# Edge step 1 of a graph network in four stages instead of three, with more buffers for the streams of step 0

## The chip, the cores and the metric

The kernel runs on one core of a Trainium2 chip. The metric is the device time in microseconds (us) of one execution. A core has five engines with their own instruction queues: TensorE (PE in the profile, and PEld for its weight loads), VectorE (DVE), ScalarE (ACT), GpSimd (POOL) and SyncE (SP). They run side by side and wait for each other through semaphores. In this kernel SP starts the plain transfers, and POOL starts the gathers, which fetch rows of a table by index.

## The reference

The network has 12,500 nodes and 412,500 edges, sorted by destination. Two graph convolutions come first; this change doesn't touch them. Then a mesh network runs: nodes and edges are encoded to 64 features, and two edge steps, each followed by a node step, update them. Cut to what matters here:

```python
e = _ln(_mlp(edge_feat, edge_enc_w0, ...))                 # edge encoder
for s in range(2):
    ce = concat([e, n[senders], n[receivers]])
    e = e + _ln(_mlp(ce, edge_blk_w0[s], edge_blk_b0[s], edge_blk_w1[s], edge_blk_b1[s]))
    agg = segment_sum(e, receivers)
    n = n + _ln(_mlp(concat([n, agg]), node_blk_w0[s], ...))
# _mlp(x) = silu(x @ w0 + b0) @ w1 + b1;  _ln is a layer norm over 64 features
```

## The kernel before

The edges are padded to 405 groups of 1,024 (8 tiles of 128). An edge step is a loop of three iterations on the device, and each iteration has 135 groups unrolled in it. `edge_step(s)` writes out, by hand, the order of the instructions on PE, DVE and ACT (`manual_schedule` names these three). SP's order is left to a planner; POOL issues the gathers in the order of the program.

For one group c the work has these stages.

- **Loads.** `send` brings the encoder's input `at` (step 0, L894) or the stored edge features `e` (step 1, L950). `send_window` brings, in four transfers of SP, the receivers' table rows `qd` (L958) and the relative destinations `rb` (L959). `ahead` has POOL issue eight gathers of 128 rows of the senders' table (L348) into the ring buffer `pg`. The ring has five buffers (R = 5), and the gathers run three groups ahead (LA = 3), so in step g POOL writes the buffer that the hidden layer of group g-2 read.
- **Hidden layer.** `hidden_blk` multiplies `e` and the receivers' part (L908) and adds the gathered rows (L910) in one PSUM bank; ACT applies Silu and writes `h` (L913). In step 0 `hidden_enc` does the same for the encoder (L899, L901).
- **Output layer.** `second` adds the bias (L918) and multiplies `h` by the second weights (L920). `normalised` squares on ACT (`sq`, L419), sums on DVE (`var`, L421), takes a reciprocal root in eleven small DVE operations (L422, L403 to L408) and scales into `y` (L427).
- **Window sum.** `window_sum` multiplies `y` by a one-hot matrix `oh` (L318) on PE (L330). DVE adds the 64-node window to the accumulator in the next step (L338).

The constants `ENC, ENC2, TURN, BLK, BLK2, SUM` say how many steps after a group's first step each stage is issued. Step 0 also encodes, so it has six stages, and in it the outputs of the encoder and of the block go through one `normalised` call with two parts (tile `sq16`). In step 1, `BLK, BLK2, SUM` are 0, 1, 2. In step g, PE therefore gets, in this order: the output layer of group g-1, the window sum of group g-2, the hidden layer of group g. ACT gets `sq` of group g-1 and then `h` of group g. DVE gets the pending window addition, the one-hot matrices `oh` and `ot` (L965), and the normalisation of group g-1.

Of the kernel before, what the change touches and what calls it, by code (L numbers as in the profile page):

```python
# [9 lines left out]
F32 = mybir.dt.float32  # L10
# [8 lines left out]
P = 128  # L19
K = 8  # L20
W = 64
D = 64
# [13 lines left out]
def gcn_then_mesh_gnn_kernel(ctx: ExitStack, tc: tile.TileContext, a: dict, out: bass.AP):  # L36
# [28 lines left out]
    KP = K // 2  # L65
# [24 lines left out]
    def bank(name):  # L90
        return psum.tile([128, 512], F32, name=f"ps_{name}")
# [23 lines left out]
    with tc.tile_pool(name="prep", bufs=2) as prep:  # L115
        ldst = prep.tile([P, NT], I32, name="ldst", bufs=1)
        nc.sync.dma_start(ldst, a["dstT"])
        for g0 in range(0, NG, P):
            n = min(P, NG - g0)
# [46 lines left out]
    with tc.tile_pool(name="sort", bufs=1) as sp, \  # L166
# [116 lines left out]
        for t, to in ((free, slot_t), (k, drel_t), (vals[turn], ew_t)):  # L283
            for j0 in range(0, NS, 4):
                n = min(4, NS - j0)
# [113 lines left out]
    def rsqrt(pool, v, shape, name):  # L399

        y = pool.tile(shape, F32, name=f"{name}_y")
        t = pool.tile(shape, F32, name=f"{name}_t")
        nc.vector.tensor_single_scalar(t.bitcast(I32), v.bitcast(I32), 1, op=OP.arith_shift_right)  # L403
        nc.vector.tensor_scalar(y.bitcast(I32), t.bitcast(I32), -1.0, MAGIC, op0=OP.mult, op1=OP.add)
        for _ in range(3):
            nc.vector.tensor_mul(t, y, y)  # L406
            nc.vector.scalar_tensor_tensor(t, t, -0.5, v, op0=OP.mult, op1=OP.mult)  # L407
            nc.vector.scalar_tensor_tensor(y, t, 1.5, y, op0=OP.add, op1=OP.mult)  # L408
        return y

    def normalised(pool, n, *parts):


        k = parts[0][0].shape[1] // D
        m = len(parts) * k
        sq = pool.tile([n, m, D], F32, name=f"sq{m}")
        v = pool.tile([n, m], F32, name=f"var{m}")
        for i, (o, _) in enumerate(parts):
            nc.scalar.activation(sq[:, i * k:(i + 1) * k, :], o.rearrange("p (k f) -> p k f", f=D),  # L419
                                 AF.Square, scale=D ** -0.5)  # L420
            nc.vector.tensor_reduce(v[:, i * k:(i + 1) * k], sq[:, i * k:(i + 1) * k, :], axis=AX.X, op=OP.add)  # L421
        nc.vector.tensor_scalar_add(v, v, EPS)  # L422
        r = rsqrt(pool, v, [n, m], f"rs{m}")
        for i, (o, y) in enumerate(parts):
            s = r[:, i * k:(i + 1) * k, None]
            o = o.rearrange("p (k f) -> p k f", f=D)
            nc.vector.tensor_tensor(y, o, s.to_broadcast(list(y.shape)), op=OP.mult)  # L427
# [25 lines left out]
    with tc.tile_pool(name="gcn", bufs=1) as gp, tc.tile_pool(name="gcnw", bufs=2) as gw:  # L453
# [209 lines left out]
        for c in range(NCH):  # L663
# [6 lines left out]
            h = gw.tile([32, CN], F32, name="h")  # L670
# [31 lines left out]
    work = first.enter_context(tc.tile_pool(name="first", bufs=2))  # L702
# [114 lines left out]
    def node_mlp(products, b0, w1, b1, update):  # L817

        ph = bank("h")
        for i, (w, v) in enumerate(products):  # L820
            nc.tensor.matmul(ph[:D, :CN], w, v, start=(i == 0), stop=(i == len(products) - 1))  # L821
        h = work.tile([D, CN], F32, name="nh")
        nc.scalar.activation(h, ph[:D, :CN], AF.Silu, bias=b0)  # L823
        po = bank("o")
        nc.tensor.matmul(po[:NP, :CB * D], ones[:, :NP], b1, start=True, stop=False)
        for b in range(CB):
            nc.tensor.matmul(po[:NP, b * D:(b + 1) * D], h[:, b * NP:(b + 1) * NP], w1[:D, :D],  # L827
                             start=False, stop=(b == CB - 1))
        y = work.tile([NP, CB, D], F32, name="ny")
        normalised(work, NP, (po[:NP, :CB * D], y))  # L830
        pt = bank("t")
        for b in range(CB):
            nc.tensor.transpose(pt[:D, b * NP:(b + 1) * NP], y[:, b, :], ident[:NP, :NP])  # L833
        update(pt[:D, :CN])
# [55 lines left out]


    def edge_inputs(col):
        at = work.tile([16, KP * P], F32, name="at")
        nc.sync.dma_start(at, a["attrT"][:, ds(col, KP * P)])  # L894
        return at

    def hidden_enc(at):
        ph = bank("h")
        nc.tensor.matmul(ph, ee_w0, at, start=True, stop=True)  # L899
        h = work.tile([128, KP * P], F32, name="h")  # L900
        nc.scalar.activation(h, ph, AF.Silu, bias=ee_b0)  # L901
        return h

    def hidden_blk(s, e, pg, more=()):

        ph = bank("h")
        for i, (w, v) in enumerate([(eb_w0[s], e), *more]):
            nc.tensor.matmul(ph, w, v, start=(i == 0), stop=False)  # L908
        for j in range(KP):
            nc.tensor.matmul(ph[:, j * P:(j + 1) * P], pg[:, 2 * j:2 * j + 2, :].rearrange("p k f -> p (k f)"),  # L910
                             ident, start=False, stop=(j == KP - 1))
        h = work.tile([128, KP * P], F32, name="h")
        nc.scalar.activation(h, ph, AF.Silu, bias=eb_b0[s])  # L913
        return h

# [15 lines left out]
    def edge_step(s):  # L931
# [2 lines left out]
        ring = [work.tile([P, K, D], F32, name=f"pg{i}", bufs=1) for i in range(R)]  # L934
        acc = (s01, 0, 128) if s == 0 else (ns2, D, D)

        ENC, ENC2, TURN, BLK, BLK2, SUM = (0, 1, 2, 3, 4, 5) if s == 0 else (None, None, None, 0, 1, 2)

        def body(it, drl, offs, ahead):
            feats, hids, hidb, y0, y1, es, windows, hots, ohs = ({} for _ in range(9))  # L940
# [3 lines left out]
            def send(g):  # L944

                if s == 0:
                    feats[g] = edge_inputs(col(g))
                else:
                    es[g] = work.tile([128, KP * P], F32, name="e", bufs=6)
                    nc.sync.dma_start(es[g], e1_d[:, ds(col(g), KP * P)])  # L950
# [22 lines left out]
            for g in range(GB + SUM + 1):  # L973
# [24 lines left out]
                if parts:  # L998
                    normalised(work, P, *parts)
# [13 lines left out]
                if s == 0 and real(g):  # L1013
                    hids[g] = hidden_enc(feats.pop(g))
                if real(g - BLK):
                    c = g - BLK
                    hidb[c] = hidden_blk(s, es[c], ring[c % R], hots.pop(c))
# [7 lines left out]
    def spread_edge_step(s):  # L1025
        def body(it, group):
# [10 lines left out]
            for g in range(GI):  # L1037
                gs = slice(g * K, (g + 1) * K)
                col = (it * GI + g) * (KP * P)
                pg = work.tile([P, K, D], F32, name="pg")  # L1040
                qg = work.tile([P, K, D], F32, name="qg")
                gather(tabs_p[s], si[:, gs], pg)
                gather(tabs_q[s], di[:, gs], qg)
                nc.vector.tensor_add(pg, pg, qg)
                e = work.tile([128, KP * P], F32, name="e")
                if s == 0:
                    y0 = ys[:, 0, gs, :]
                    normalised(work, P, (second(hidden_enc(edge_inputs(col)), *ee1), y0))
                    nc.scalar.activation(e, turned(y0), AF.Identity, scale=e_g[0])
                    y = ys[:, 1, gs, :]  # L1050
                else:
                    nc.sync.dma_start(e, e1_d[:, ds(col, KP * P)])
                    y = ys[:, gs, :]
                normalised(work, P, (second(hidden_blk(s, e, pg), *eb1[s]), y))
                if s == 0:
                    nc.vector.scalar_tensor_tensor(e, turned(y), e_g[1], e, op0=OP.mult, op1=OP.add)
                    nc.sync.dma_start(e1_d[:, ds(col, KP * P)], e)
                group(g, val)
# [8 lines left out]
    for s in range(2):  # L1067
        with tc.tile_pool(name=f"edges{s}", bufs=2) as work:
            edge_step(s)
        with tc.tile_pool(name=f"spread{s}", bufs=2) as work:  # L1070
            spread_edge_step(s)
        with tc.tile_pool(name=f"nodes{s}", bufs=2) as work:
            for c in range(NCH):
                node_step(s, c)
                if s == 0:
                    send_tables(1, c)
                else:
                    decode(c)
# [45 lines left out]
```

## Time and profile before

| what | value |
|---|---|
| three runs, median | 18249.7 us (18242.7 to 18254.52) |
| profiled execution: its own time, its span | 18269.4 us, 18267.6 us |
| mean granted TensorE clock | 0.804 |
| edge step 0 with its loads | about 6020 to 12420 us |
| edge step 1 with its loads | about 12750 to 17780 us |
| share of the span: PE, PEld, DVE, POOL, ACT | 70%, 53%, 50%, 34%, 13% |

The profile describes one execution. A row of its costliest groups gives the line, the engine, the operation, what it writes and reads, how often it ran, its busy time and mean duration, and then the idle time of that engine just before it with what ended most of that idle time. "remote" as what ended a wait means that a semaphore moved, but that no instruction or transfer in the profile ended near that moment; on one core it is not another core. "issue" means that the profile shows no wait at all. The ends of matmuls are modelled, not observed.

### The profile page before, as it was taken

To read this page: it belongs to the slowest core of one execution; us is meant where nothing else is said; L and a number is where in the kernel's file an instruction comes from. 1 tells how busy PE (TensorE), PEld (TensorE's weight loads), DVE (VectorE), ACT (ScalarE), POOL (GpSimd) and SP (SyncE) were. 2 spreads that over 40 slices of the span, in tenths; PEclk is the share of its full clock that TensorE was granted. 3 is DMA by queue.
4 is the path that set the end of the run, shared out by engine and by line. 5 is a ranking of instruction groups with operands and counts; after the bars stand their busy time and mean duration, and the time that the engine had idled before them with its cause. 6 is when DMAs were issued, how large, how long until landed. Compare 5 with 4: busy or idle time off the path is not lost. (4 is left out here: it accounts for less than half of the span.)

```text
span 18267.6 us, 286566 instructions
## 1 busy us (share of the span) xinstructions
PE 12803.6 (70%) x107075; PEld 9720.4 (53%) x107682; DVE 9165.7 (50%) x23663; ACT 2363.3 (13%) x3705; POOL 6263.8 (34%) x6572
## 2 busy tenths in 40 slices
PE   0179999899995677777777777777555555555556
PEld 0169999699994444454444444443434343433432
DVE  9967777577775344444444444443333333333332
ACT  3300000000001112222222122221111111111110
POOL 0000000000000444454444444441666666666650
PEclk9989999899995777777777777775777777777775
DMA  0011111111111112221212222222222222222230
GB/s 25 7 13 61 58 56 56 42 56 57 53 62 27 46 46 48 47 52 47 46 46 47 49 48 48 48 48 45 61 58 58 59 58 58 58 58 58 58 51 2
DMA packets 1008981, 877.55 MB, mean 48 GB/s; under 512 B 650695, under 2 KB 755755, under 8 KB 1006879
## 3 DMA queue, kind: packets, MB, share of 16 engines
q1 hardware_dynamic: 798640, 644.15, 12.1%
q0 software_dynamic: 208896, 214.33, 7.4%
q8 instruction: 884, 14.48, 0.3%
q14 instruction: 561, 4.59, 0.1%
HBM read 723.20 MB, written 134.51 MB: 47 GB/s over the span
## 5 line engine op out<-in xcount | busy, mean ns | idle before, releaser
L348 POOL DMA_INDIRECT pg<-tab_p,si_cur x6480 | 6209.5, 958 | 5153.3 <-PE ps_h L910 2936.8
L920 PE MATMUL ps_o<-eb_w,h 128*128 128x128 f32 x6480 | 1193.0, 340 | 2167.0 <-ACT h L913 1639.6
L552 PE MATMUL ps_h<-t,roh 128*128 128x128 bf16 x39936 | 2541.4, 220 | 234.4 <-DVE roh L531 234.4
L552 PEld LDWEIGHTS <-roh 128*128 128x128 bf16 x39936 | 2395.3, 99 | 284.1 <-DVE roh L531 238.3
L421 DVE TENSOR_REDUCE var<-sq 128x8 f32<-128x512 f32 (+1 forms) x1290 | 857.5, 668 | 2943.5 <-ACT sq L419 2118.8
L920 PEld LDWEIGHTS ps_o<-eb_w,h 128*128 128x128 f32 x6480 | 1008.1, 237 | 2384.6 <-ACT h L913 1748.7
L330 PE MATMUL ps_seg<-oh,y 128*64 128x64 f32 x19440 | 1482.8, 250 | 1017.3 <-issue 993.4
L348 POOL DMA_INDIRECT pg<-tab_p,si_fst x48 | 45.5, 947 | 5452.9 <-DVE offs L368 5438.9
L568 PE MATMUL ps_seg<-ohd,msg 128*128 128x112 f32 x13312 | 1850.4, 280 | 0.0
L330 PEld LDWEIGHTS ps_seg<-oh,y 128*64 128x64 f32 x19440 | 1199.8, 160 | 1155.2 <-issue 1113.2
L965 DVE TENSOR_SCALAR ot<-rb,iop 128x512 bf16<-128x512 bf16 x810 | 303.4, 375 | 2657.0 <-DMA rb<-relg_d 2224.2
L568 PEld LDWEIGHTS ps_seg<-ohd,msg 128*128 128x128 f32 x13312 | 1628.2, 192 | 0.0
L559 DVE TENSOR_TENSOR msg<-ps_h,wm 128x512 f32<-128x512 f32 (+1 forms) x1792 | 1166.2, 651 | 722.8 <-PE ps_h L552 711.8
L908 PE MATMUL ps_h<-e,eb_w 128*128 128x512 f32 x1620 | 1401.1, 954 | 147.7 <-issue 82.1
L910 PEld LDWEIGHTS ps_h<-ident,pg 128*128 128x128 f32 x6480 | 1108.7, 241 | 252.9 <-issue 162.3
L556 DVE TENSOR_TENSOR ohd<-ior,rdrel 128x448 f32<-128x448 f32 (+1 forms) x1792 | 1056.3, 590 | 276.0 <-PE ps_seg L568 249.0
L913 ACT ACTIVATE h<-ps_h,eb_b 128x512 f32<-128x512 f32 x810 | 556.4, 687 | 4865.1 <-remote 2996.3
L910 PE MATMUL ps_h<-ident,pg 128*128 128x128 f32 x6480 | 1086.8, 322 | 39.2 <-issue 35.6
L419 ACT ACTIVATE sq<-ps_o 128x512 f32<-128x512 f32 (+1 forms) x1290 | 754.2, 585 | 2148.4 <-issue 680.3
L899 PE MATMUL ps_h<-at,ee_w 16*128 16x512 f32 x810 | 703.4, 928 | 426.4 <-issue 351.8
L908 PEld LDWEIGHTS <-qd 128*128 128x128 bf16 x2430 | 306.7, 127 | 1022.8 <-issue 973.5
L427 DVE TENSOR_TENSOR y<-ps_o,rs_y 128x512 f32<-128x512 f32 x1215 | 802.3, 687 | 89.9 <-issue 4.1
(247 smaller groups left out, 12454.2 us busy)
## 6 DMA issues: line engine op xcount, KB each, us to landing
mod<-mod_d SPq DMA_DIRECT2D x256, 832.0 KB
pg<-tab_p,si_cur POOLq DMA_INDIRECT x6480
rb<-relg_d SPq DMA_DIRECT2D x1620, 64.0 KB
e_d<-e SPq DMA_DIRECT2D x405, 256.0 KB
e<-e_d SPq DMA_DIRECT2D x405, 256.0 KB
qd<-tab_q SPq DMA_DIRECT2D x1620, 24.0 KB
at<-in_attrT SPq DMA_DIRECT2D x405, 32.0 KB
tab_q<-tabs SPq DMA_DIRECT2D x50, 187.5 KB
```

What stands on the lines that cost most here:

```text
L330: nc.tensor.matmul(ps[r:r + n, :W], v, oh[:, k, :], start=(k == 0), stop=(k == K - 1))
L348: nc.gpsimd.indirect_dma_start(out=to[:, k, :], out_offset=None, in_=table, in_offset=bass.IndirectOffsetOnAxis(ap=idx[:, k:k + 1], axis=0))
L419: nc.scalar.activation(sq[:, i * k:(i + 1) * k, :], o.rearrange("p (k f) -> p k f", f=D), AF.Square, scale=D ** -0.5)
L421: nc.vector.tensor_reduce(v[:, i * k:(i + 1) * k], sq[:, i * k:(i + 1) * k, :], axis=AX.X, op=OP.add)
L427: nc.vector.tensor_tensor(y, o, s.to_broadcast(list(y.shape)), op=OP.mult)
L552: nc.tensor.matmul(pg[:, (j - j0) * SB * F:(j - j0 + 1) * SB * F], ohs[h][:, u, at * P:(at + 1) * P], t3[:, i, u, b:b + SB * F], start=(i ...
L556: nc.vector.tensor_tensor(ohd[:, :n, :], ior[:, None, :].to_broadcast([P, n, LR]), drel[:, j0:j0 + n, r:r + 1].to_broadcast([P, n, LR]), o ...
L559: nc.vector.tensor_tensor(msg[:, :n * SB, :], pg[:, :n * SB * F].rearrange("p (s f) -> p s f", f=F), wm[:, j0:j0 + n, :].rearrange("p j s ...
L568: nc.tensor.matmul(acc[:SB * F, :LR], msg[:, j * SB:(j + 1) * SB, :].rearrange("p s f -> p (s f)"), ohd[:, j, :], start=(j0 + j == 0), sto ...
L908: nc.tensor.matmul(ph, w, v, start=(i == 0), stop=False)
L910: nc.tensor.matmul(ph[:, j * P:(j + 1) * P], pg[:, 2 * j:2 * j + 2, :].rearrange("p k f -> p (k f)"), ident, start=False, stop=(j == KP - 1))
L920: nc.tensor.matmul(po[:, j * 128:(j + 1) * 128], h[:, j * P:(j + 1) * P], w1, start=False, stop=(j == KP - 1))
```

## The change

The changed kernel does three things.

- In edge step 1 the stages become `BLK, BLK2, SUM = 0, 2, 3`. In step g, PE gets the output layer of group g-2, the window sum of group g-3 and the hidden layer of group g. The loop over steps is one longer in each of the three iterations.
- The tile `h` gets three buffers instead of two, in both functions that allocate it, since two hidden layers now wait while a third is written.
- The encoder's input `at` (used in step 0 alone) gets four buffers instead of two, and the squares of a two-part call (`sq16`, step 0 alone) get one instead of two. The squares of a one-part call keep two.

```diff
-        sq = pool.tile([n, m, D], F32, name=f"sq{m}")
+        sq = pool.tile([n, m, D], F32, name=f"sq{m}", bufs=1 if m > K else 2)
...
-        at = work.tile([16, KP * P], F32, name="at")
+        at = work.tile([16, KP * P], F32, name="at", bufs=4)
...
     def hidden_enc(at):
...
-        h = work.tile([128, KP * P], F32, name="h")
+        h = work.tile([128, KP * P], F32, name="h", bufs=3)
...
     def hidden_blk(s, e, pg, more=()):
...
-        h = work.tile([128, KP * P], F32, name="h")
+        h = work.tile([128, KP * P], F32, name="h", bufs=3)
...
-        ENC, ENC2, TURN, BLK, BLK2, SUM = (0, 1, 2, 3, 4, 5) if s == 0 else (None, None, None, 0, 1, 2)
+        ENC, ENC2, TURN, BLK, BLK2, SUM = (0, 1, 2, 3, 4, 5) if s == 0 else (None, None, None, 0, 2, 3)
```

## The prediction

> **What bounds the kernel now.** I read the slices of the page first: edge step 0 fills about 6020 to 12420 us of the span and edge step 1 about 12750 to 17780 us. The stages change only in step 1, so I asked for the busy times in three stretches inside its iterations. The columns are PE, PEld, DVE, ACT and POOL, each with its count, then clock, DMA share and GB/s:
>
> ```profile
> 13000.00:14400.00 1400.00, 765.61 (x4275) 561.62 (x4331) 528.22 (x1935) 145.46 (x227) 881.73 (x909) 0.75 0.26 58
> 14500.00:16000.00 1500.00, 827.04 (x4569) 604.23 (x4631) 563.69 (x2066) 156.37 (x244) 945.39 (x975) 0.75 0.26 58
> 16200.00:17700.00 1500.00, 806.21 (x4542) 594.40 (x4602) 562.58 (x2057) 155.88 (x243) 942.91 (x970) 0.76 0.27 58
> ```
>
> The reader is to see the pace. 909 + 975 + 970 = 2854 gathers in 4400 us are 356.75 groups of eight, so a group takes **12.33 us**, 405 of them 4994 us. No engine is full: POOL is busiest, at 63%.
>
> Then the groups of instructions between 13000 and 17700 us (379 groups of edges):
>
> ```profile
> L348 POOL DMA_INDIRECT pg<-tab_p,si_cur x3032 | 2943.6, 971 | 1719.5 <-issue 800.2 <-PE ps_h L910 462.6 <-remote 446.7
> L920 PE MATMUL ps_o<-eb_w,h 128*128 128x128 f32 x3036 | 657.3, 384 | 2037.3 <-ACT h L913 1547.5 <-issue 469.6 <-ACT sq L419 20.1
> L913 ACT ACTIVATE h<-ps_h,eb_b 128x512 f32<-128x512 f32 x379 | 260.3, 687 | 3213.4 <-remote 2746.2 <-PE ps_h L910 256.0 <-issue 190.0
> ```
>
> PE stands idle 2037.3 / 379 = **5.38 us** per group ahead of the output layer, waiting for `h`; its other work takes 12.33 - 5.38 = 6.95 us. POOL stands idle 1719.5 us ahead of gathers. The ordinary gap between two gathers is 0.30 us (the timeline below), 910 us over 3032, so 810 us or **2.14 us** per group are real pauses. POOL's own pace without them is 12.33 - 2.14 = 10.2 us.
>
> Why `h` is late is in the timeline:
>
> ```profile
> 15513.61 1.40 POOL L348 DMA_INDIRECT pg<-tab_p,si_cur  x1 [2.25 <-remote]
> 15514.30 2.08 PE L920 MATMUL ps_o<-eb_w,h 128*128 128x128 f32 x8 [5.66 <-ACT h L913]
> 15516.30 1.97 PE L330 MATMUL ps_seg<-oh,y 128*64 128x64 f32 x16
> 15520.86 1.05 PE L910 MATMUL ps_h<-ident,pg 128*128 128x128 f32 x8
> ...
> 15531.53 0.69 ACT L913 ACTIVATE h<-ps_h,eb_b 128x512 f32<-128x512 f32 x1 [14.52 <-remote]
> ...
> 15532.27 2.07 PE L920 MATMUL ps_o<-eb_w,h 128*128 128x128 f32 x8 [10.04 <-ACT h L913]
> ...
> 15538.38 1.05 PE L910 MATMUL ps_h<-ident,pg 128*128 128x128 f32 x8
> 15539.04 0.94 POOL L348 DMA_INDIRECT pg<-tab_p,si_cur  x1 [5.08 <-PE ps_h L910]
> ```
>
> The hidden layer's matmuls are over at 15521.9, but ACT may start only at 15531.53: 9.6 us later, with nothing else in its way. Over the trace these late releases come only when POOL has issued gathers for some 6 us without a pause; the lag averages 4.9 us a group in step 1 and 0.1 us in step 0, where POOL rests 6 us a group. So a pause of POOL lets PE's releases through, and PE's release lets POOL go on. At 15531.5 the chain `h`, output, sum, hidden layer (7.5 us) runs before POOL's next release at 15539.04: that is the 5.08 us pause.
>
> **What the Trainium skill says.** "Perfetto Trace Analysis", section "Tensor Engine Instruction (MATMUL, LD_WEIGHTS)": the end of a matmul is an estimate, and the semaphore is sent only after PSUM has acknowledged the write. The trace agrees that a modelled end is no release, but at 15539.53 ACT starts 0.10 us after the last L910 (15538.38 + 1.05), so the 9.6 us are no acknowledgement. The same page, "DMA Instruction — SWDGE (GPSIMD)": a gather's interval ends with its descriptors, not with the data. So POOL's 0.94 us is issuing time; in this stretch the data is not late (waits for `pg` sum to under 4 us). "TensorE: Matmul & The Clock Gate", "What's actually happening": after an idle window of about 3.4 us the array runs at half clock. The trace agrees: the eight matmuls of L920 take 2.08 us after a 5.66 us wait, but 1.16 us at 15540.27 after a 0.52 us wait.
>
> **The change part by part.**
>
> *Output layer one step later.* PE still issues the same instructions per group. The wait of 5.38 us ahead of L920 loses its cause: `h` of group g-2 was started a whole step earlier. Of the 5.38 us ACT itself takes 0.7; the rest is late release. If nothing took its place, PE would need 6.95 us a group, and POOL would bound. What the program can gain is therefore POOL's pauses at most: 2.14 x 405 = 867 us.
>
> Which pauses go? I counted POOL's runs between pauses over 0.8 us, from 12800 to 17700 us: 195 runs of eight gathers followed by a pause of 2.29 us on average (12.1 us a group); 51 runs of sixteen followed by 4.48 us; and 39 runs of fourteen and two, with pauses of 1.22 and 4.84 us. These hold 3000 of some 3130 gathers. The long pauses are the chain above, 7.5 us after a late release. With the change the next hidden layer doesn't wait for `h`, and so has mostly been done by the time the release comes; I shorten these to the 2.29 us of the short ones: 51 x (4.48 - 2.29) + 39 x (1.22 + 4.84 - 2.29) = 112 + 147 = **259 us**. The 2.29 us pauses I leave, since they are what lets a release through, not PE's work. Bounds: no gain (0), and all pauses gone (867).
>
> *Window sum one step later.* It stays one step behind the output layer. It needs `y`, so ACT `sq` 0.60, `var` 0.69, eleven small operations at 0.20, `y` 0.69: 4.2 us, and 1.26 us of L338, L318 and L965, which DVE does first: 5.5 us. Between the two PE now has a sum, a hidden layer and an output layer, about 6.9 us. It fits by 1.4 us; a release of L920 that is late by 4.9 us would make PE wait 3.5 us there. That keeps PE at 10.5 us a group, near POOL's 10.2, so I charge nothing, and hold the rest in the rivals.
>
> *One step more at the end of each iteration*: three times at most PE's 6.95 us, **+21 us**. Its loads and gathers are not more.
>
> *`h` with three buffers* follows the later reader; no instruction changes. Cost 0.
>
> *`at` with four buffers (step 0).* SP waits there for L899, 3045 us (and 871 "remote") in the queue's own waits, and `qd`, `rb` stand behind it; DVE waits 2119.6 us for `rb` ahead of L965. These waits go. In the order built from the changed kernel the store of `e` comes ahead of the last `rb` load of a window, two steps ahead of its use. But PE is what orders step 0: its whole wait for DVE's `y` is under 30 us there, and DVE's next work, `var`, waits for PE's outputs anyway (`ot` at 9509.81, `sq` on ACT at 9510.60, `var` at 9511.23). Value 0; if that cover fails, 0.15 us a group either way, ±60 us.
>
> *`sq16` with one buffer (step 0).* The next square comes some 14 us after the last reduction of the old one (9512.86 and 9527.84). Cost 0, and up to 405 x 0.1 = 40 us if ACT were made to wait.
>
> *Sum*: -259 + 21 = **-238 us**. Against the profiled execution's 18269.4 us this gives 18031; it stands 20 us above the median, so against the median 18249.7 - 238 = **18012 us**.
>
> **The rivals.**
>
> *A. Pauses go more widely.* PE gets a group or more ahead, releases are always there in time, and half or all of the 2.29 us pauses vanish as well: another 195 x 2.29 / 2 = 223 us and more, so 17400 to 17790. For it: PE's 6.95 us against 10.2. Against it: without pauses no release comes early.
>
> *B. The wait moves.* The late release of L920 now holds `sq`, `y` and the window sum back by what `h` cost before; the idle time stands ahead of L330, the pace stays 12.3 us: 18250 ± 35.
>
> *C. Slower.* PE no longer stops POOL after eight gathers, so POOL issues sixteen in a row everywhere, and PE's issue and releases starve for longer. In step 0 this is seen: about 5 to 6 us into POOL's run the matmuls of L330 come 1.4 us apart. A pair of fourteen and two costs 16 x 1.25 + 1.22 + 4.84 = 26.1 us, 13.0 a group. If all groups went so, +0.7 x 405 = 283 us, 18530; half of them, 18390. It decides as soon as the double runs grow beyond the 90 counted while their pauses stay at 4.5 us or more.
>
> That the change doesn't do what it says has little room: in the order built from it, each L920 of step 1 stands a hidden layer later.
>
> **How the numbers follow.** My case has 0.50, A 0.17, B 0.13, C 0.20. My case's own range is 17800 to 18210. Leaving a tenth out at each end, the range reaches into A and into C: **17650 to 18390 us**. A measurement of this kernel can tell about 0.2% (36 us) from no change. Faster by more: 0.50 + 0.17 + a little of B = **0.69**; within: **0.10**; slower: 0.20 + a little of B = **0.21**.
>
> **What would show it.** Right: the idle time ahead of L920 falls from 5.38 to under 2 us a group, POOL's pauses from 2.14 to about 1.5, the pace to 11.7 us, step 0 unchanged to 1%. Wrong towards B: the same microseconds ahead of L330. Wrong towards C: more double runs, a pace over 12.4 us. A pace near 10.2 us, or a step 0 that moves by over 60 us, would show that I mis-sized a part.

## The result, and the profile after

The changed kernel takes 18567.43 us (median of four runs, 18559.77 to 18576.78), the kernel before 18252.11 us (four runs, 18242.7 to 18259.46). The ratio is **1.0173, 95% interval 1.0156 to 1.0191**: slower by 1.73%, 315 us, where 18012 us had been forecast and 18390 us was the upper end of the range.

The pace of each edge step tells where the time went. It is the time from the last hidden-layer matmul (L910) of an iteration's first group to that of its last, over 134 groups, taken from the trace and averaged over the three iterations.

| us per group | before | after | difference over 3 x 134 groups |
|---|---|---|---|
| edge step 0 | 15.65 | 16.79 | +455 us |
| edge step 1 | 12.34 | 11.88 | -185 us |

Between the iterations of step 1 and after its last group the changed kernel takes 9 + 18 us more. 455 - 185 + 27 = 297 us, and the two profiled executions differ by 18561.6 - 18267.6 = 294 us of span. So step 1 did gain, and **step 0, where the stages are as before, lost two and a half times as much.**

Three rows of the page of before, then the same of after (count, then busy time, mean ns, then the idle time ahead and what ended most of it):

```profile
L348 POOL DMA_INDIRECT pg<-tab_p,si_cur x6480 | 6209.5, 958 | 5153.3 <-PE ps_h L910 2936.8
L920 PE MATMUL ps_o<-eb_w,h 128*128 128x128 f32 x6480 | 1193.0, 340 | 2167.0 <-ACT h L913 1639.6
L330 PE MATMUL ps_seg<-oh,y 128*64 128x64 f32 x19440 | 1482.8, 250 | 1017.3 <-issue 993.4
```

```profile
L348 POOL DMA_INDIRECT pg<-tab_p,si_cur x6480 | 6179.6, 954 | 5464.2 <-PE ps_h L910 3026.5
L330 PE MATMUL ps_seg<-oh,y 128*64 128x64 f32 x19440 | 1577.9, 241 | 1981.6 <-issue 1923.1
L920 PE MATMUL ps_o<-eb_w,h 128*128 128x128 f32 x6480 | 1135.7, 311 | 706.2 <-issue 684.6
```

L920 had 2167.0 us of idle time ahead of it before, most of it waiting for `h`; that is now 706.2 us, and `h` is no longer named. L330, the window sum, had 1017.3 us, and has 1981.6. For "issue" the profile shows nothing that PE waited for: its instructions simply start late.

Step 1 alone, in three stretches inside its iterations (columns as in the prediction), and its groups of instructions between 13300 and 18000 us (392 groups of edges):

```profile
13400.00:14700.00 1300.00, 792.68 (x4116) 538.77 (x4168) 516.22 (x1865) 134.93 (x218) 845.28 (x877) 0.72 0.26 60
15000.00:16300.00 1300.00, 793.43 (x4100) 539.21 (x4155) 515.72 (x1864) 135.16 (x218) 844.77 (x879) 0.72 0.26 60
16600.00:17900.00 1300.00, 800.85 (x4122) 541.49 (x4177) 516.22 (x1856) 134.68 (x218) 844.62 (x878) 0.72 0.27 60
```

```profile
L348 POOL DMA_INDIRECT pg<-tab_p,si_cur x3136 | 3021.2, 963 | 1624.0 <-issue 840.1 <-remote 537.8 <-PE ps_h L910 111.4
L330 PE MATMUL ps_seg<-oh,y 128*64 128x64 f32 x6272 | 658.4, 263 | 463.4 <-issue 419.6 <-DVE y L427 31.8 <-DVE rs_y L408 9.7
L920 PE MATMUL ps_o<-eb_w,h 128*128 128x128 f32 x3140 | 636.6, 330 | 690.8 <-issue 674.2 <-ACT h L913 14.2
L910 PE MATMUL ps_h<-ident,pg 128*128 128x128 f32 x3136 | 569.1, 309 | 472.6 <-issue 446.8 <-DMA pg<-tab_p,si_cur 23.1
```

2634 gathers in 3900 us are 329.25 groups, 11.84 us each (12.33 before). PE's idle time ahead of L920 is 690.8 / 392 = 1.76 us a group instead of 5.38. But 1.18 us stand ahead of L330 and 1.21 us ahead of L910; in the kernel before these were 74.0 / 396 = 0.19 and 0.02.

**Step 0** is read from three views. First the window sum among PE's groups of instructions between 6500 and 11800 us, before and then after:

```profile
L330 PE MATMUL ps_seg<-oh,y 128*64 128x64 f32 x10670 | 647.3, 230 | 785.5 <-issue 782.5
```

```profile
L330 PE MATMUL ps_seg<-oh,y 128*64 128x64 f32 x9957 | 689.3, 230 | 1149.1 <-issue 1145.5
```

A group has 32 of these matmuls in step 0, so the counts are 333.4 and 311.2 groups, and the idle time ahead of the window sum rose from 2.36 to 3.69 us a group. That alone is more than the 1.13 us by which the pace rose.

Second, what SP's queue waited for in the same stretch, before and after (us in total, times, longest), and DVE's row L965, before and after:

```profile
SPq L894 <- PE ps_h L899: 2608.9, 232, 13.2
SPq L894 <- remote: 729.6, 72, 11.3
```

```profile
SPq L894 <- PE ps_h L899: 2840.1, 283, 11.3
SPq L958 <- PE ps_h L910: 883.0, 299, 14.0
```

```profile
L965 DVE TENSOR_SCALAR ot<-rb,iop 128x512 bf16<-128x512 bf16 x333 | 131.8, 396 | 1931.6 <-DMA rb<-relg_d 1812.4 <-issue 46.6 <-PE ps_o L920 40.3
L965 DVE TENSOR_SCALAR ot<-rb,iop 128x512 bf16<-128x512 bf16 x312 | 110.0, 352 | 1120.1 <-PE ps_h L908 1106.9 <-DMA rb<-relg_d 6.6 <-issue 6.6
```

SP still waits for L899 ahead of `at` (L894). With four buffers it is two groups further ahead, and so its next load, `qd` (L958), now finds its own buffer unread: it waits some 3 us in nearly every group for the hidden layer's matmuls. There are four buffers of `qd`, and L908 has to have read the oldest. The kernel before met that wait once in this stretch, for 5.8 us. DVE no longer waits for `rb` (1812.4 us before, 6.6 after), but now for the matmuls L908.

Third, the timeline of one group, without the rows of other engines. Before, the five transfers of a group are issued ahead of POOL's run of eight gathers, which starts at 8307.18:

```profile
8304.09 0.60 SPq L958 DMA_DIRECT2D qd<-tab_q  x1
8304.89 0.48 SPq L959 DMA_DIRECT2D rb<-relg_d  x1
...
8307.08 0.39 SPq L1010 DMA_DIRECT2D e_d<-e  x1
8307.18 0.94 POOL L348 DMA_INDIRECT pg<-tab_p,si_cur  x1 [8.11 <-PE ps_h L910]
...
8311.77 1.48 PE L330 MATMUL ps_seg<-oh,y 128*64 128x64 f32 x29
...
8315.10 0.22 PE L330 MATMUL ps_seg<-oh,y 128*64 128x64 f32 x1 [0.48 <-issue]
```

After, four of the five are issued inside the run:

```profile
8399.67 0.57 SPq L958 DMA_DIRECT2D qd<-tab_q  x1
...
8400.33 0.94 POOL L348 DMA_INDIRECT pg<-tab_p,si_cur  x1 [6.05 <-PE ps_h L910]
8400.50 0.47 SPq L959 DMA_DIRECT2D rb<-relg_d  x1
8401.23 0.39 SPq L1010 DMA_DIRECT2D e_d<-e  x1
...
8401.82 0.59 SPq L958 DMA_DIRECT2D qd<-tab_q  x1
8402.62 0.76 SPq L959 DMA_DIRECT2D rb<-relg_d  x1
...
8404.75 0.91 PE L330 MATMUL ps_seg<-oh,y 128*64 128x64 f32 x23
...
8412.01 0.46 PE L330 MATMUL ps_seg<-oh,y 128*64 128x64 f32 x2 [0.45 <-issue]
```

In both, PE's window sum starts at full speed and then becomes slow, with a step of 0.7 us or a multiple of it between instructions, until a little after POOL's run has ended. Before, 29 of the matmuls are through first, and the sum takes 3.6 us (8311.77 to 8315.32); what is left of the slow stretch falls on the next matmuls, L899. After, 23 are through, and it takes 7.7 us.

These are single groups. Counted over 399 groups of step 0 in each trace, 1.4 of the five transfers start inside POOL's run (from the start of its first gather to the end of its eighth) on average before, and 4.0 after. Before, none starts inside it in 146 groups; after, four do in 383. So the reader sees a wait that went (DVE's for `rb`), a wait that stayed (SP's for L899), a wait that came (SP's ahead of `qd`), and a slow stretch of PE that grew. What connects them is for the experiments.

### The profile page after: what moved, and what is told of

Read it like the earlier page. It is cut to its first block, busy times and chain, and to the rows that moved or that the text cites. A ratio compares the mean times of both kernels' runs of the same rounds, so it can differ in the third digit from the quotient of the medians.

```text
span 18561.6 us, 285828 instructions
## 1 busy us (share of the span) xinstructions
PE 13050.5 (70%) x107078; PEld 9690.0 (52%) x107682; DVE 9202.6 (50%) x23663; ACT 2348.6 (13%) x3705; POOL 6233.8 (34%) x6572
## 3 DMA queue, kind: packets, MB, share of 16 engines
q1 hardware_dynamic: 798640, 644.15, 11.8%
## 5 line engine op out<-in xcount | busy, mean ns | idle before, releaser
L330 PE MATMUL ps_seg<-oh,y 128*64 128x64 f32 x19440 | 1577.9, 241 | 1981.6 <-issue 1923.1
L330 PEld LDWEIGHTS ps_seg<-oh,y 128*64 128x64 f32 x19440 | 1203.9, 150 | 2168.6 <-issue 2069.8
L920 PE MATMUL ps_o<-eb_w,h 128*128 128x128 f32 x6480 | 1135.7, 311 | 706.2 <-issue 684.6
L910 PEld LDWEIGHTS ps_h<-ident,pg 128*128 128x128 f32 x6480 | 1152.2, 242 | 746.8 <-issue 647.5
L908 PE MATMUL ps_h<-e,eb_w 128*128 128x512 f32 x1620 | 1468.8, 1002 | 91.2 <-DMA e<-e_d 53.6
L910 PE MATMUL ps_h<-ident,pg 128*128 128x128 f32 x6480 | 1146.4, 319 | 499.2 <-issue 472.6
L920 PEld LDWEIGHTS ps_o<-eb_w,h 128*128 128x128 f32 x6480 | 930.3, 211 | 1007.2 <-issue 979.0
L965 DVE TENSOR_SCALAR ot<-rb,iop 128x512 bf16<-128x512 bf16 x810 | 288.3, 356 | 1830.8 <-PE ps_h L908 1438.9
L899 PE MATMUL ps_h<-at,ee_w 16*128 16x512 f32 x810 | 782.0, 1055 | 397.2 <-issue 330.8
L908 PE MATMUL ps_h<-ot,qd 128*128 128x512 bf16 x1827 | 792.9, 536 | 240.2 <-issue 164.3
L908 PEld LDWEIGHTS <-qd 128*128 128x128 bf16 x2430 | 326.7, 135 | 1151.8 <-issue 1101.5
```

Source lines behind the costliest of these rows:

```text
L330: nc.tensor.matmul(ps[r:r + n, :W], v, oh[:, k, :], start=(k == 0), stop=(k == K - 1))
L920: nc.tensor.matmul(po[:, j * 128:(j + 1) * 128], h[:, j * P:(j + 1) * P], w1, start=False, stop=(j == KP - 1))
```

## The experiments

**Theory L**: the loss lies in step 0, comes from the four buffers of `at`, and comes through SP's new wait ahead of `qd`, by which a group's transfers are issued in POOL's run instead of ahead of it. **Rival M**: any way of running two groups further ahead costs the same. **Rival S1**: the four stages, `h` or the squares cost it. A further question was how far all of it rests on PE's slow stretches during POOL's runs (theory S) rather than on a cost of the buffers' own.

The runs fell on chips other than that of the result, and the chips differ much: the kernel before, run beside each group of runs, took 17648.73 us on one (called B here), 17723.51 us on another (D), and 15059.55 to 15076.16 us in five groups on three others (C). Only ratios to the kernel before on the same chip, and paces on the same chip, are compared. On B and D the times of one kernel scatter by up to 1%, so the pace, which is of one profiled execution, carries less there than the median.

### The parts of the change (chip B)

Four stages and three `h`, with `at` and `sq16` at two buffers:

```diff
-        sq = pool.tile([n, m, D], F32, name=f"sq{m}", bufs=1 if m > K else 2)
+        sq = pool.tile([n, m, D], F32, name=f"sq{m}")
-        at = work.tile([16, KP * P], F32, name="at", bufs=4)
+        at = work.tile([16, KP * P], F32, name="at")
```

> Only the four stages of step 1, with h in three buffers; at keeps two buffers and sq16 two. Theory 1 (the changed kernel loses in step 0 through the four buffers of at, and gains in step 1 through the stages): step 0 stays at 15.65 us a group, step 1 takes 11.9, total 18,060 to 18,080 us. Theory 2 (the loss comes from the single buffer of squares): the same here. Theory 3 (the loss comes from h in three buffers): step 0 at 16.8 us a group, total about 18,570 us.

The changed kernel with only `at` back at two buffers (the second pair of lines above):

> The changed kernel with at back in two buffers; sq16 keeps its one buffer. Theory 1: step 0 back to 15.65 us a group, total 18,060 to 18,080 us. Theory 2 (single buffer of squares): step 0 stays at 16.8, total about 18,570 us.

The kernel before with `at` at four buffers and `sq16` at one, the old stages:

> The kernel before with at in four buffers and sq16 in one [...]; stages and h as before. Theory 1: step 0 at 16.8 us a group, step 1 at 12.34, total about 18,710 to 18,760 us, and the run with at undone shows that it is at. If step 0 suffers only together with h in three buffers, 18,250 us.

| kernel | us | ratio, 95% interval | step 0, step 1, us per group |
|---|---|---|---|
| stages alone | 17573.62 | 0.995 (0.9929 to 0.9971) | 14.68, 11.78 |
| changed, `at` two | 17546.37 | 0.9938 (0.9916 to 0.9961) | 14.67, 11.76 |
| old stages, `at` four, `sq16` one | 17964.7 | 1.0192 (1.0167 to 1.0217) | 15.12, 12.05 |

The stages gain 0.5%. One buffer of squares costs nothing: the first two rows differ only in it and their intervals overlap. Four buffers of `at` cost 1.9% without the stages, in step 0. (The paces give 0.45 us a group, 181 us; the median of the third row lies 316 us above the kernel before. The profiled executions of the first two rows were the slowest of theirs, 102 and 117 us above their medians, and that of the third the fastest, 35 us below.) That refutes S1 on this chip. PE's idle time ahead of L330 in step 0 (7000 to 9400 us) moves with it: 272.2 us for 162 groups with `at` two, 358.7 us for 155.1 groups with `at` four, 1.68 and 2.31 us a group.

### Breaking POOL's run (chip B)

The changed kernel with `at` at two buffers, and in step 0 POOL makes four copies (128x512 words, 0.63 us each) after the fourth gather of each group. POOL's order is then written by hand too, in both steps (not in this excerpt of the edit):

```diff
             def ahead(g):
-                gather(table, si_cur[:, g * K:(g + 1) * K], ring[(g + LA) % R])
+                to, idx = ring[(g + LA) % R], si_cur[:, g * K:(g + 1) * K]
+                for k in range(K):
+                    nc.gpsimd.indirect_dma_start(...)
+                    if k + 1 in (4,) and rest:
+                        for _ in range(4):
+                            nc.gpsimd.tensor_copy(spare, si_cur[:, :512])
```

> The run with at undone, and in step 0 POOL rests after the fourth gather of each eight: four small copies, some 2 us in all. Theory P (while POOL issues gathers for more than 5 us without a rest, PE's instructions and releases starve): the 1.4 us gaps of L330 in step 0 go or shrink from 2.3 us a group to under 1, and PE then also runs at a better clock; step 0 at 12.5 to 14.5 us a group, total 500 to 1,200 us below the run with at undone. Rival (the gaps are PE's own, such as its instruction supply at this point of the loop): step 0 unchanged within 1%, the gaps stay at the same place after L928.

16894.5 us, ratio 0.9578 (0.956 to 0.9596): 4.2% faster than the kernel before and **3.7% faster than the same kernel without copies (17546.37 us), with more work on POOL.** Step 0 takes 12.78 us a group instead of 14.67, step 1 is unchanged at 11.77. POOL's groups of instructions between 6500 and 11000 us, in this kernel:

```profile
L378 POOL DMA_INDIRECT pg<-tab_p,si_cur x2775 | 2670.1, 962 | 855.7 <-issue 776.6 <-PE ps_h L919 30.7 <-PE ps_h L917 6.9
L383 POOL COPY spare<-si_cur 128x512 int32<-128x512 int32 x1388 | 872.3, 628 | 65.1
```

POOL hardly waits for PE any more (30.7 us for L919, which is L910 here; in the run with `at` two it was 1513.4 us over the same stretch). It is now POOL that sets the pace: 8 gathers and their gaps, 8 x (2670.1 + 855.7) / 2775 = 10.2 us, and four copies, (872.3 + 65.1) / 347 groups = 2.7 us. PE's window sum and the encoder's matmul (L899, here L908) in that stretch, first with `at` two, then with the copies:

```profile
L330 PE MATMUL ps_seg<-oh,y 128*64 128x64 f32 x9632 | 530.0, 229 | 511.9 <-issue 508.5
L899 PE MATMUL ps_h<-at,ee_w 16*128 16x512 f32 x603 | 478.6, 844 | 227.4 <-issue 197.9 <-DMA qd<-tab_q 24.0
```

```profile
L330 PE MATMUL ps_seg<-oh,y 128*64 128x64 f32 x11072 | 663.5, 238 | 609.0 <-issue 605.3
L908 PE MATMUL ps_h<-at,ee_w 16*128 16x512 f32 x692 | 521.8, 841 | 31.4 <-DMA qd<-tab_q 25.0 <-issue 6.3
```

The pace lies in the range expected, and the rival (unchanged within 1%) fails. But one part of the expectation missed: the idle time ahead of L330 doesn't shrink to under 1 us a group, it stays at 1.76 us (1.70 with `at` two). What goes is the idle time behind the sum, 0.75 to 0.09 us ahead of the encoder's matmul, and PE's busy time falls from 3541.22 / 301 = 11.8 us a group to 3743.03 / 346 = 10.8, at a granted clock of 0.85 instead of 0.79. The timeline shows where the slow stretch now ends:

```profile
8008.69 0.74 PE L330 MATMUL ps_seg<-oh,y 128*64 128x64 f32 x17
...
8010.39 0.34 PE L330 MATMUL ps_seg<-oh,y 128*64 128x64 f32 x3 [0.96 <-issue]
...
8011.58 2.69 POOL L383 COPY spare<-si_cur 128x512 int32<-128x512 int32 x4
...
8013.25 0.72 PE L330 MATMUL ps_seg<-oh,y 128*64 128x64 f32 x8 [1.08 <-issue]
```

The window sum becomes slow late in the run and is fast again some 1.7 us after the copies have begun: the last eight matmuls take 0.72 us together. Over all groups of step 0, more than 99% of L330's gaps over 0.3 us, by time, lie before the point 2 us after the copies' start. So what slows PE goes with POOL's uninterrupted issuing of gathers, not with POOL being busy.

### The same questions on chips where nothing is slow (C)

Six buffers of `qd` in the changed kernel:

```diff
-    qd = [wp.tile([128, 3, 128], BF16, name=f"qd{i}") for i in range(4)]
+    qd = [wp.tile([128, 3, 128], BF16, name=f"qd{i}") for i in range(6)]
```

> The changed kernel with six buffers of `qd` instead of four; all else as changed (`at` four, `sq16` one, `h` three, four stages). With four buffers of `at`, SP runs two groups further ahead, and its `qd` load then waits for the matmul L908 that reads the old one, so that SP's transfers of a group start together with POOL's run of gathers instead of just ahead of it. Theory L (the loss of step 0 comes from where these transfers stand against POOL's run): without that wait they move ahead of the run again, and step 0 falls back to the pace that it has with two buffers of `at`; ratio to the kernel before 0.990 to 0.998. Rival M (the loss comes from being further ahead in any way, or from the buffers' places): step 0 keeps its pace of the changed kernel; ratio 1.014 to 1.020. Step 1 unchanged under both, 11.8 us a group.

The changed kernel with POOL's copies (128x448 words) after the fourth gather in step 0:

> The changed kernel (`at` with four buffers), and in step 0 POOL makes four copies of 128x448 words, some 2.3 us, after the fourth gather of each group. Theory P (four buffers of `at` cost time only through POOL's long runs, during which PE and SP are served late): the loss vanishes with the rest, step 0 runs at POOL's own 8 x 1.25 + 2.3 = 12.3 us a group, ratio 0.945 to 0.965. Rival (the buffers cost PE or DVE something of their own): about 1.1 us a group above that, 13.4 us, ratio 0.972 or more. Step 1 unchanged, 11.8 us.

The copies after the eighth gather instead, in both steps (`at` two):

> Four stages with `at` at two buffers, and POOL's copies after the eighth gather of a group instead of the fourth: four in step 0 (2.5 us), two in step 1 (1.3 us). The same work on POOL in another place. Theory P1 (what counts is where the rest falls in PE's group: it must fall into the window sum): step 0 goes back towards 14.6 us a group, or over it, as the copies lie where POOL waited anyway; ratio about 0.99 to 1.00. Theory P2 (what counts is that POOL's own pace is a little slower than PE's, so that POOL never waits for PE's release and PE never for POOL): the place doesn't matter, step 0 takes 8 x 1.25 + 2.7 = 12.8 us as with the copies after the fourth, ratio 0.955 to 0.965. In step 1 P2 gives 8 x 1.25 + 1.3 = 11.3 to 11.5 us, P1 11.8 to 12.3.

Two copies after the fourth gather, in both steps (`at` two):

> Four stages with `at` at two buffers, and two copies (1.3 us) after the fourth gather of each group in both steps. If POOL's own pace sets the group once it has rests, step 0 takes 8 x 1.25 + 1.3 = 11.3 us unless PE's own work, 11.4 us busy a group in the run with four copies, becomes the bound: 11.4 to 12.2 us. Step 1: 11.3 to 11.5 us if the pauses at PE's late releases go, 11.8 if they stay, 13 if rest and pauses add. Ratio 0.92 to 0.945 in the first case. Rival: 1.3 us are too short a rest, the late releases stay, and step 0 stays above 13.5 us, ratio 0.97 or more.

These four ran on a chip of kind C. The first two ran twice more, again on chips of kind C:

> The changed kernel with six buffers of `qd` instead of four, once more, since the kernel before ran in 15059.64 us on the chip of the last group and its gathers bound both steps there without a pause. Where the kernel before takes 17600 us or more, so that PE is served late in POOL's runs: theory L (the loss comes from SP's transfers of a group starting together with POOL's run instead of ahead of it, because `qd` waits for L908): step 0 back to its pace with two buffers of `at`, ratio 0.990 to 0.998. Rival M (the loss comes from SP being further ahead in any way): ratio 1.014 to 1.020. Where it takes some 15060 us, 0.997 to 0.999 again, and neither is told apart.

> The changed kernel with four copies of 128x448 words by POOL after the fourth gather of each group of step 0, once more. Where the kernel before takes 17600 us or more: theory P (four buffers of `at` cost time only through POOL's long runs): step 0 at POOL's own pace, 12.1 us as on the other chip, ratio 0.935 to 0.965; rival (the buffers cost PE or DVE something of their own): 13.2 us or more, ratio over 0.97. Where the kernel before takes some 15060 us, 1.06 again, since the copies only add to the engine that bounds it.

> The changed kernel with six buffers of `qd`, again for a chip on which the kernel before takes 17600 us or more. There theory L (SP's transfers of a group collide with POOL's run because `qd` waits for L908) expects 0.990 to 0.998 and a pace of step 0 as with two buffers of `at`; rival M (being further ahead costs by itself) 1.014 to 1.020. On a chip where the kernel before takes some 15060 us, 0.997 once more.

> The changed kernel with POOL's four copies of 128x448 words after the fourth gather of each group of step 0, again for a chip on which the kernel before takes 17600 us or more. There theory P (four buffers of `at` cost time only through POOL's long runs) expects step 0 at 12.1 us, ratio 0.935 to 0.965; the rival (a cost of their own) 13.2 us or more, over 0.97. Where the kernel before takes some 15060 us, 1.06 once more.

With them ran the changed kernel as it is, six `qd` beside it, and the old stages with `at` four:

> The changed kernel as it is, on another chip than its first runs. Theory S (its loss needs PE to be served late during POOL's runs, as on the chip of the result): where the kernel before takes 18250 or 17650 us, ratio 1.010 to 1.020, step 0 about 1 us a group over the kernel before. Where the kernel before takes some 15060 us, its gathers bound both steps at 9.82 us a group and neither the stages nor the buffers matter: 0.996 to 1.003. Rival (four buffers of `at` cost PE or DVE something of their own wherever they run): slower by over 1% on every chip.

> The changed kernel with six buffers of `qd`, beside the changed kernel on the same chip. Where the kernel before takes 17600 us or more: theory L (SP's transfers of a group collide with POOL's run, because `qd` waits for L908): 1.5% or more below the changed kernel, 0.990 to 0.998 of the kernel before; rival M (being further ahead costs by itself): within 0.3% of the changed kernel. Where it takes some 15060 us: both 0.997 to 1.000.

> Three stages as before, with four buffers of `at` and one of `sq16`: the part that lost 1.9% in the first group of runs. Theory S (the loss needs PE to be served late in POOL's runs): 0.998 to 1.001 where the kernel before takes some 15060 us, since the gathers bound both steps there; 1.015 to 1.022 where it takes 17600 us or more. Rival (the buffers cost something of their own everywhere): over 1.01 on every chip. With it, the changed kernel's 0.9955 there falls to the stages: theory S then leaves 0.995 to 0.998 for them, in the bounds between the iterations, since the pace is POOL's.

> The changed kernel with six buffers of `qd`, beside the run with four buffers of `at`. Where the kernel before takes 17600 us or more: theory L (SP's transfers of a group collide with POOL's run because `qd` waits for L908) 0.990 to 0.998, with step 0 at its pace with two buffers of `at`; rival M (being further ahead costs by itself) 1.014 to 1.020. Elsewhere 0.997 once more.

| kernel (kind C) | us | ratio, 95% interval | step 0, step 1, us per group |
|---|---|---|---|
| changed | 15007.76 | 0.9955 (0.9938 to 0.9972) | 9.81, 9.85 |
| old stages, `at` four, `sq16` one | 15047.44 | 0.9989 (0.998 to 0.9998) | 9.82, 9.94 |
| changed, six `qd` | 15025.65 | 0.9977 (0.9968 to 0.9986) | 9.84, 9.82 |
| the same, four more times | 15021.57 to 15035.35 | 0.9971 to 0.9978 | 9.86 to 9.87, 9.82 to 9.85 |
| changed, copies in step 0 | 15971.14 | 1.0606 (1.0588 to 1.0623) | 12.14, 9.84 |
| the same, two more times | 15975.29, 15962.5 | 1.0597, 1.0597 | 12.16 and 12.14, 9.85 |
| copies after the eighth, both steps | 16597.29 | 1.102 (1.1002 to 1.1038) | 12.40, 11.11 |
| two copies after the fourth, both | 15971.46 | 1.0607 (1.0589 to 1.0625) | 10.97, 11.01 |

Here **the change is faster by 0.45%** (0.9955, just under the 0.996 to 1.003 expected), and the four buffers of `at`, which lose 1.9% on chip B, lose nothing. Six buffers of `qd` are 27 us slower than four beside them on the same chip (15034.68 and 15007.76 us). The page of the changed kernel on such a chip:

```profile
L348 POOL DMA_INDIRECT pg<-tab_p,si_cur x6480 | 6168.8, 952 | 2008.7 <-issue 1268.3
L910 PE MATMUL ps_h<-ident,pg 128*128 128x128 f32 x6480 | 1175.9, 300 | 1545.0 <-DMA pg<-tab_p,si_cur 1541.3
L920 PE MATMUL ps_o<-eb_w,h 128*128 128x128 f32 x6480 | 1177.2, 337 | 3.4 <-ACT h L913 3.4
L330 PE MATMUL ps_seg<-oh,y 128*64 128x64 f32 x19440 | 1108.1, 242 | 29.3 <-DVE y L427 29.3
```

A gather takes as long as on the chip of the result, 952 ns against 954. But POOL's idle time is hardly more than the 0.30 us gap of 6480 gathers (1944 us), both steps run at its 9.8 us a group, and PE waits for the gathered rows (1541.3 us ahead of L910). There is no slow stretch: the idle time ahead of L330 is 29.3 us in all, and none of it is "issue". The Trainium skill ("Perfetto Trace Analysis", "DMA Instruction — SWDGE (GPSIMD)") says that a gather's interval ends with its descriptors and not with the data; here the trace agrees: in 70 waits of L910 for `pg` in step 0, PE starts 1.5 to 2.6 us after the row of the last gather that it needs has ended. The stages gain here too: with `at` four in both, the four stages are 15047.44 - 15007.76 = 40 us faster than the three (two chips of the kind, with the kernel before at 15062.49 and 15076.16 us), and the wait of L920 for `h` falls from 178.1 us with three stages to 3.4.

What the copies do here tells the other half. POOL is the bound, so they add their own time, 4 x 0.57 us to 9.8 in the first row of copies and 2 x 0.62 to 9.8 in the last. The gains that were expected of them didn't come. Whether copies take away the loss by `at`, whether their place matters, and how short they may be stays open for a chip like that of the result: none of these kernels ran on one.

### Six buffers of `qd` where PE is served late (chip D)

> The kernel before, unchanged, to have its profile on another chip. Theory S: where it takes some 15060 us, PE has no slow stretch in the window sum L330 (idle time ahead of it under 0.3 us a group, 2.3 us on the chip of the result), ACT's h follows PE's last L910 at once although POOL issues without a pause, and the gathers bound both steps at some 9.8 us a group. Rival (the chips differ in transfers or in the clock alone): the same waits as on the chip of the result, all shorter in proportion.

> The changed kernel with six buffers of `qd`. Where the kernel before takes 17600 us or more: theory L (SP's transfers of a group collide with POOL's run because `qd` waits for L908) 0.990 to 0.998; rival M (being further ahead costs by itself) 1.014 to 1.020. Elsewhere 0.997 once more.

| kernel (chip D) | us | ratio, 95% interval | step 0, step 1, us per group |
|---|---|---|---|
| the kernel before, again | 17715.64 | 0.9986 (0.9969 to 1.0003) | 14.68, 12.07 |
| changed, six `qd` | 17739.23 | 1.0011 (0.9996 to 1.0026) | 14.72, 11.91 |

The page of the kernel before on chip D, to be read beside the four lines of kind C:

```profile
L348 POOL DMA_INDIRECT pg<-tab_p,si_cur x6480 | 6207.4, 958 | 4657.5 <-PE ps_h L910 2550.4
L920 PE MATMUL ps_o<-eb_w,h 128*128 128x128 f32 x6480 | 1214.7, 345 | 1913.1 <-ACT h L913 1447.3
L330 PE MATMUL ps_seg<-oh,y 128*64 128x64 f32 x19440 | 1414.7, 250 | 825.7 <-issue 801.8
```

The gathers are as long (958 ns), but PE has its slow stretches (801.8 us of "issue" ahead of L330), ACT starts `h` in step 1 on average 4.3 us after PE's last L910 (0.1 us in the old stages on kind C, under gathers that don't pause at all), and POOL waits for PE. This fits theory S, and not a difference in transfers or in the clock alone, in which every wait would have shrunk in proportion. Another reading speaks against that rival. Ahead of the edge steps, from 1000 to 5500 us, where POOL issues no gather, PE is busy for 4242.46 us in the kernel before on the chip of the result, 4244.62 us on D and 4244.25 us in the old stages on kind C, each at a granted clock of 0.96. PE may also be without a wait because it lacks instructions; but the transfers of 16 KB in the queue of instructions (q8, 7000 to 9400 us) are no longer where PE is slow, 1.10 us on the chip of the result and 1.11 us on kind C. Whether they start late stays open.

With six buffers of `qd` the wait of SP ahead of L958 is gone from the queue's waits, which in step 0 (6500 to 11800 us) are headed by:

```profile
SPq L894 <- PE ps_h L899: 1765.7, 178, 13.0
SPq L894 <- remote: 1136.8, 115, 11.2
```

In the timeline the transfers stand ahead of POOL's run again: `qd` at 8300.67, the store of `e` at 8303.72, the first gather at 8303.76. Step 0 takes 14.72 us a group, as in the kernel before on the same chip (14.68). That profiled execution of the kernel before was the slowest of ten, though. From the medians (17739.23 - 17723.51 = 16 us, although step 1 gains 0.16 x 402 = 65 us and loses 15 at its ends), step 0 loses an estimated (16 + 50) / 402 = 0.16 us a group. The idle time ahead of L330 in step 0, for the kernels without copies:

| chip | kernel | us of idle time ahead of L330 per group, step 0 | worked out from |
|---|---|---|---|
| of the result | before; after | 2.36; 3.69 | shown above |
| B | `at` two; `at` four | 1.68; 2.31 | shown above |
| D | before; six `qd` with `at` four | 1.69; 1.72 | 599.9 and 610.2 us for 355 groups each |

The ratio of 1.0011 lies outside the ranges of both L (0.990 to 0.998) and M (1.014 to 1.020). Against M the pace of step 0 decides: `at` has its four buffers, DVE's `ot` (L965) waits for L908 as in the changed kernel (618.3 us in 5300, there 1106.9), and yet step 0 loses 0.04 to 0.16 us a group. L has step 0 right; its total missed because step 1 gained 0.16 us a group here and not the 0.3 by which three and four stages differ on chip B (12.05 and 11.76); why, stays open. **So the loss by `at` is tied to SP's wait ahead of `qd`, if the changed kernel loses on D what it loses elsewhere.** That is inferred from two other chips, as the changed kernel itself didn't run on D; and what two more buffers of `qd` may change beside that wait, such as where other buffers lie, no run tells apart.

That it acts through the transfers' place in POOL's run is not shown by an experiment: no kernel moved the transfers without touching that wait. The traces support it in part. With `at` two, 2.3 of the five transfers start inside POOL's run on chip B, with `at` four 4.0; on D it is 2.2 in the kernel before and 2.3 with six `qd`. And within the kernel before, on the chip of the result, groups with none of the five inside (146) take 15.84 us, those with four inside (27) 17.25 us, about the 17.04 us of the 383 such groups after. But the 20 groups with all five inside take 13.76 us. So the four-inside pattern, in which the changed kernel is held, is the slow one, and "inside or ahead" alone is too simple a rule.

No version was best everywhere. On chip B, where PE is served late, the four stages with the copies after the fourth gather gain 4.2%; on the other kind such copies cost 6%, and there the changed kernel is the fastest of those run.

## Why the prediction was wrong

Point by point, by its own steps.

- **What bounds the kernel: right on the chip it was read from.** Late releases by PE in POOL's runs and POOL's pauses for PE set the pace. On kind C, where neither is seen, POOL's 9.8 us bound both steps; the profile of one chip couldn't tell.
- **Output layer one step later: right in mechanism, the term too large.** Idle time ahead of L920 fell from 5.38 to 1.76 us (forecast: under 2). POOL's real pauses fell from 2.14 to (1624.0 - 3136 x 0.30) / 392 = 1.74 us a group (forecast about 1.5), the pace to 11.84 to 11.88 (forecast 11.7), and the gain was 185 us instead of 259. The step that was mis-sized is the length of the long pauses. I let all of them shrink to 2.29 us. In the trace after, the 39 pairs of fourteen and two are down to 8, but there are 113 runs of sixteen instead of 51, and their pause is still 4.02 us. The release still comes late (ACT starts `h` 5.2 us after the last L910 on average, 4.9 before), and what waited at L920 stands in part at L330 and L910 (1.18 and 1.21 us a group).
- **One more step per iteration: right.** 21 us forecast, 27 measured (9 between the iterations, 18 after the last).
- **The window sum one step later: nearly free,** but not at 0: the 1.0 us a group that L330's idle time grew by in step 1 is in the pace above.
- **`h` with three buffers, `sq16` with one: right,** no cost that the runs on chip B could tell.
- **`at` with four buffers: the step that failed.** I valued it at 0, and at 0.15 us a group should the cover fail. Step 0 became 1.13 us a group longer, 455 us, and the runs on chip B show that the buffers of `at` alone lose time there. I said which waits would go. DVE's for `rb` went; SP's for L899 did not (2608.9 us before, 2840.1 after). I said that PE orders step 0, so that waits of SP and DVE are covered. PE indeed hardly waits for DVE's `y`, and the conclusion is wrong all the same. I didn't ask which buffer SP would stop at next: two groups further ahead it is `qd`, four buffers deep and released by L908. And I took PE's own time in step 0 as fixed, though the prediction itself describes PE's slow stretch there. That stretch grew: the idle time ahead of L330 went from 2.36 to 3.69 us a group. That it grew through SP's new wait is argued from the traces and from chip D; no run on the chip of the result shows it. My own words named the sign: "or a step 0 that moves by over 60 us, would show that I mis-sized a part."
- **The rivals.** C had the right sign and half of the right mechanism (PE starved in POOL's run), but placed it in step 1 through double runs. Those did become more (113), yet they cost less than I charged, 12.08 us a group and not 13.0. B holds in part: some of the wait moved to L330.

## What to carry to other kernels

A deeper buffer moves its queue to the next wait: before a buffer is valued at nothing, work out which buffer the queue stops at next, who releases that one, and what the transfers behind it will then run beside. Where an engine's own instructions turn slow with nothing to wait for ("issue") while another engine does something, don't take that time for fixed work: here it grew with a change of buffers elsewhere. And run a change of this size on more than one chip: here the same edit was 1.7% slower on one and 0.45% faster on another.

## What the hardware showed that was not expected

- The same program took 18252 us, 17649 us, 17724 us and some 15060 us on different chips. On three chips of the last kind POOL issued gathers through a whole iteration without a pause, and neither late releases nor slow stretches of PE appeared; on the others, gathers of the same length (952 to 958 ns) went with both. What makes the chips differ, these runs don't show.
- Where it happens, it begins 5 to 9 us into an unbroken run of gathers (in most groups of step 0, on three chips): instructions of PE then come 0.7 us or a multiple of it apart, and in step 1 ACT starts on average 4.3 us (D) or 4.9 us (the chip of the result) after PE's last matmul, not 0.1. On chip B, copies by POOL in the middle of the run end it within 2 us of their start, and POOL working 2.7 us more in a group of step 0 made the group 1.9 us shorter.
